# A graph layer with gathered rows on one core: the row gathers are made to wait for TensorE, and the two node tables are made in one pass

## The chip, the cores and the metric

The kernel runs on one core of a Trainium2 chip. The metric is the time on the device in microseconds (us), as the median of several runs. One execution was taken by the hardware profiler; its lines below name the engines PE (TensorE matmul), PEld (TensorE weight load), DVE (VectorE), ACT (ScalarE), POOL (GpSimd) and SP (SyncE). Every matmul of float32 shows as two matmuls and two weight loads in the trace, so counts of matmuls are twice those of the code.

## The reference: one message-passing layer

There are 6250 nodes with 128 features and 100000 edges, sorted by destination.

```python
msg_in = concatenate([x[src], x[dst], edge_features], axis=1)     # 128 + 128 + 4
h = silu(msg_in @ mW1 + mb1)
aggregated = segment_sum(h @ mW2 + mb2, dst, num_segments=N)
u = silu(concatenate([x, aggregated], axis=1) @ uW1 + ub1)
x = layernorm(x + layer_norm(x + u @ uW2 + ub2, ln_g, ln_b))
```

## The kernel before: two tables, then 98 groups of edges

**Split.** The first product is split by rows of mW1. Table A is x times the source part and table B is x times the destination part plus the bias. Both are written to DRAM (tab_a, tab_b), 49 tiles of 128 nodes each, in seven parts of up to eight tiles. Since the sum over edges is linear, h is summed per node first, and mW2 is folded into the node stage with a count of edges per node, deg.

**Start (L274 to L388).** POOL gathers the source rows of an edge group with `fetch(g)`: eight indirect DMAs of 128 rows each (L277). The first RAW = 4 groups are gathered from x itself, so that they need not wait for tab_a. PE turns x (`turn_x`, L330), multiplies part by part for A (`table(i0, n, 0)`, L350), ScalarE copies the result (L365), and SP writes it. After all of A come the destination lists, then the raw rows are turned (`turn_rows`, L357) and B is made part by part (L382) and written.

**Edge groups.** An edge group has 1024 edges in eight tiles; there are NG = 98. The destinations of one group span at most W = 96 nodes. Iteration g of the main loop runs, in the order written by hand for SP, PE, DVE and ACT:

- `fetch(g + AHEAD)` with AHEAD = 4 (POOL), and `load(g + 4)`, two short DMAs on SP (L553, L554)
- `hidden(g)`: VectorE adds the gathered rows to the product in PSUM (L598, tile s) and ScalarE applies silu (L599, tile h)
- `products(g + 2)`: PE, eight matmuls of the 96 B rows and the four edge features with a one-hot matrix (L583); raw groups add a product with the turned rows (L585)
- `node_matrix(g + 3)` and `edge_matrix(g + 1)`: the two one-hot matrices on VectorE (L558, L571). The first also leaves the group's degrees in a column of deg_g
- `add(g - 2)`: the sums and the degrees of the group are added to acc and deg (L622)
- `by_nodes(g)`: PE transposes the column of degrees (`degrees`, L604) and sums h per node with eight matmuls (L609, tile pt)

Every eighth group or so, a node batch of four tiles is threaded through the loop in steps (L476 to L526). The last two batches follow the last group.

**What orders the gathers.** POOL's order is not written by hand; a scheduler places its instructions, and the queue then runs in that order. The row tiles ga come from a pool of AHEAD + 2 = 6 buffers. A gather of group k therefore waits for the reader of group k - 6, which is the VectorE add L598 (for raw groups the products L585). Nothing else holds a gather back.

Of the kernel before, what the change touches and what calls it, by code (L numbers as in the profile page):

```python
# [8 lines left out]
F32 = mybir.dt.float32  # L9
# [9 lines left out]
P = 128  # L19
# [5 lines left out]
def kernel(  # L25
# [40 lines left out]
    nc = tc.nc  # L66
    N, H = x.shape
# [4 lines left out]
    G = 8  # L72
# [4 lines left out]
    NW = NP + W  # L77
    K1 = W + ED
    RB = 14
    AHEAD = 4  # L80
    LEAD = 4
    RAW = 4
    MADE = 3
    NQ = 4
    NM = 5
# [12 lines left out]
        return [(i, min(g, n - i)) for i in range(0, n, g)]  # L98


    LAST = 2
    batches = []
    first = (NT - 2 * LAST) % BT
# [5 lines left out]

    edges = ExitStack()  # L110
    edges.enter_context(tc.manual_schedule(engines={ENG.SP, ENG.PE, ENG.DVE, ENG.Activation}))
    gath = edges.enter_context(tc.tile_pool(name="gath", bufs=AHEAD + 2))
    work = edges.enter_context(tc.tile_pool(name="edge", bufs=2))

    tables = ExitStack()
# [3 lines left out]
    def wide():  # L119
        return tables_ps.tile([P, G, P], F32, name="wide")  # L120
# [67 lines left out]


    acc = consts.tile([P, NW], F32, name="acc")  # L190
    deg = consts.tile([1, NW], F32, name="deg")
    deg_g = consts.tile([W, NG], F32, name="deg_g")


    src_i = consts.tile([P, NG, G], I32, name="src_i")
# [18 lines left out]
    src_n = work.tile([P, GE], F32, name="s")[:NG]  # L214
    nc.vector.tensor_copy(src_n, src_l)
    by_lane(src_i, src_n)

    def destination_lists():
        base_c = work.tile([NG, 1], F32, name="base_c", bufs=1)
# [49 lines left out]
    def tiles_of(g):  # L269
        return min(G, -(-(E - g * GE) // P))  # L270

    def fetch(g):
        if g >= NG:
            return  # L274
        rows[g] = gath.tile([P, G, H], F32, name="ga")
        for i in range(tiles_of(g)):
            nc.gpsimd.indirect_dma_start(  # L277
                out=rows[g][:, i, :],
                out_offset=None,
                in_=x if g < RAW else tab_a[:, :],  # L280
                in_offset=bass.IndirectOffsetOnAxis(
                    ap=src_i[:, g, i : i + 1] if g else src_0[:, i : i + 1], axis=0
                ),
            )

    for g in range(RAW):
        fetch(g)


    turn = edges.enter_context(tc.tile_pool(name="turn", bufs=1))  # L290
# [29 lines left out]
    def by_node(t):  # L320
        return t[:NP].rearrange("(i p) f -> p i f", p=P)
# [5 lines left out]
    def turn_x(i0, n):  # L327
        pt = wide()
        for i in range(n):
            nc.tensor.transpose(pt[:, i, :], x_sb[:, i0 + i, :], ident)  # L330
        nc.scalar.copy(xT[:, i0 * P : (i0 + n) * P], pt[:, :n, :].rearrange("p i f -> p (i f)"))

    def load_bases(g):
        _, vals = nc.values_load_multi_w_load_instructions(
# [7 lines left out]
            bases[g + k] = v  # L342

    parts = groups(NT, G)

    def table(i0, n, half):
        pm = wide()
        for j in range(n):
            cols = slice((i0 + j) * P, (i0 + j + 1) * P)
            nc.tensor.matmul(pm[:, j, :], xT[:, cols], w1[:, half, :], start=True, stop=True)  # L350
        return pm[:, :n, :]
# [8 lines left out]
    turn_x(*parts[0])  # L360
    for k, (i0, n) in enumerate(parts):
        if k + 1 < len(parts):
            turn_x(*parts[k + 1])
        ta = tpool.tile([P, G, H], F32, name="t", bufs=2)
        nc.scalar.copy(ta[:, :n], table(i0, n, 0))  # L365
# [3 lines left out]
        nc.vector.memset(deg[:, cols], 0.0)  # L369
    for t in mv:  # L370
        nc.sync.dma_start(t[W:], mW1[2 * H :])
    attributes(0)
    destination_lists()
    attribute_rows(0)
    destinations(0)
    load_bases(0)
    for k, (i0, n) in enumerate(parts):
        if k < RAW:
            turn_rows(k)

        tb = x_sb[:, i0 : i0 + n, :]
        nc.vector.tensor_add(tb, table(i0, n, 1), b1[:, None, :].to_broadcast([P, n, H]))  # L382
        nc.sync.dma_start(by_node(tab_b)[:, i0 : i0 + n, :], tb)
    if E < NG * GE:
        pad = tpool.tile([ED, NG * GE - E], F32, name="pad")
        nc.vector.memset(pad, 0.0)
# [10 lines left out]


    w2u = consts.tile([P, H], F32, name="w2u")
    mb2u = consts.tile([1, H], F32, name="mb2u")  # L400
# [21 lines left out]
    def fuse_weights():  # L422
        pm = node_y()
        nc.tensor.transpose(pm[:, 0, :], raw_w["w2"], ident)
        w2T = work.tile([P, P], F32, name="w2T", bufs=1)
        nc.scalar.copy(w2T, pm[:, 0, :])
        nc.tensor.matmul(pm[:, 1, :], w2T, raw_w["u1a"], start=True, stop=True)
        nc.tensor.matmul(pm[0:1, 2, :], raw_w["mb2"], raw_w["u1a"], start=True, stop=True)
        nc.scalar.copy(w2u, pm[:, 1, :])
        nc.scalar.copy(mb2u, pm[0:1, 2, :])  # L430


    def node_batch(i0, n, work, new, y, final=False):
# [29 lines left out]
        sums, counts = acc[:, cols], deg[:, cols]  # L463
        if not final:

            acc_b, deg_b = new("acc_b"), new("deg_b", 1)
# [89 lines left out]
    def node_matrix(g):  # L556

        nc.vector.tensor_scalar(  # L558
            stbuf[g % NST][:W],
            near.pop(g),  # L560
            p_next,
            0.0,
            op0=OP.is_equal,
            op1=OP.add,
            accum_out=deg_g[:, g : g + 1],
        )

    def edge_matrix(g):
# [7 lines left out]
        )  # L576
        return oh

    def products(g):
        pre = rows_ps()  # L580
        st = stbuf[g % NST].rearrange("k (i c) -> k i c", i=G)
        for i in range(tiles_of(g)):
            nc.tensor.matmul(pre[:, i, :], st[:, i, :], mv[g % NM], start=True, stop=g >= RAW)  # L583
# [17 lines left out]

    def degrees(g):
        pt = ps.tile([P, 2 * W], F32, name="pt")
        nc.tensor.transpose(pt[0:1, W:], deg_g[:, g : g + 1], ident[:W, :W])  # L604
        return pt

    def sums(g, pt, h, oh, lo, hi):
        for i in range(lo, hi):
            nc.tensor.matmul(  # L609
                pt[:, :W], h[:, i, :], oh[:, i, :], start=i == 0, stop=i == tiles_of(g) - 1  # L610
            )

    def by_nodes(g, h, oh):

# [2 lines left out]
        return pt  # L617

    def add(g, pt):
        for to, of in ((acc, pt[:, :W]), (deg, pt[0:1, W:])):  # L620
            at = to[:, bass.ds(bases[g], W)]
            nc.vector.tensor_add(at, at, of)  # L622

    for g in range(LEAD):
        load(g)
# [4 lines left out]
    for g in range(NG):  # L630
        if g == 3:
            load_weights()
        if g == 4:
            destination_checks(node_y())
        if g == 5:
            fuse_weights()
        for c in range(1, NC):
            if g == max(1, c * EC // GE - 10):
                attributes(c)
            if g == max(1, c * EC // GE - 10) + 1:  # L640
                attribute_rows(c)
        if g + AHEAD >= RAW:
            fetch(g + AHEAD)
        if g + LEAD < NG:
            load(g + LEAD)
        last = g >= NG - 1
        if not last:
            h[g] = hidden(g)
        if g + 2 < NG:
            pre[g + 2] = products(g + 2)  # L650
        if g + MADE < NG:
            node_matrix(g + MADE)
        if g + 1 < NG:
            oh[g + 1] = edge_matrix(g + 1)
        if g - 2 in pt:
            add(g - 2, pt.pop(g - 2))
        if last:
            break
        pt[g] = by_nodes(g, h.pop(g), oh.pop(g))
        if g >= NG - 3:  # L660
            add(g - 1, pt.pop(g - 1))
        for i0, n, first in batches[:-1]:
            if g == (first if first >= NG - 3 else first + 1):
                running.append(node_batch(i0, n, *node_tiles(nodes, node_y)))
        for _ in range(2 if g >= NG - 6 else 1):
            advance(running)
# [58 lines left out]
def general(tc, tab_a, tab_b, src_i, rel, base_p, ea_d, p_col, ident, mW1, acc, deg):  # L725
# [9 lines left out]
    with ExitStack() as es:  # L735
# [84 lines left out]
        for i in range(NP // P):  # L820
            part = keep.tile([P, WR], F32, name="part")
            nc.sync.dma_start(part, sums[i * P : (i + 1) * P])
            p_s = ps.tile([P, P], F32, name="p_s")
            nc.tensor.transpose(p_s, part[:, :H], ident)
            nc.vector.tensor_copy(acc[:, i * P : (i + 1) * P], p_s)
            p_d = ps.tile([1, P], F32, name="p_d")
            nc.tensor.transpose(p_d, part[:, H : H + 1], ident)
            nc.vector.tensor_copy(deg[:, i * P : (i + 1) * P], p_d)


# [31 lines left out]
```

## Time and profile before

| | |
|---|---|
| three runs, median (lowest to highest) | 1332.58 us (1326.24 to 1334.16) |
| the profiled execution | 1330.48 us |
| its span, first to last instruction | 1328.7 us |
| granted TensorE clock, mean | 0.659 of full speed |
| gathers on POOL (L277), x782 | 739 us busy, 0.94 us each |
| edge products (L583), x1564 matmuls | 290.6 us busy, 0.33 us each |
| node sums (L609), x1564 matmuls | 285.4 us busy, 0.32 us each |
| DMA, mean | 67 GB/s |

Busy times are sums over an engine's instructions; matmuls are pipelined, so a matmul's own time is longer than the distance to the next. A row of waits reads: engine, tile and line that waited, what released it, total us, times, longest. "issue" as a releaser means that the engine waited for nothing that the profile shows; "remote" that the releaser could not be named.

### The profile page before, as it was taken

The numbers are of one execution on the slowest core, as the hardware profiler recorded it, in microseconds if no ns is written. First come the engines' busy times: TensorE is split into PE (matmuls) and PEld (weight loads), VectorE is DVE, ScalarE is ACT, GpSimd is POOL, SyncE is SP. The second block draws the span as 40 slices with busy tenths as digits, with TensorE's granted clock in tenths as the row PEclk, the third lists the DMA queues.
The fourth block names the chain that finished last, engine by engine and source line by source line (L and its number), as shares of the span: only waits on it lengthen the run. The fifth ranks groups of instructions, "written<-read, shape, count | busy, mean of one in ns | idle before, by whom it ended". The sixth has DMA issues, their size and how long they took to land.

```text
span 1328.7 us, 11483 instructions
## 1 busy us (share of the span) xinstructions
PE 719.1 (54%) x3802; PEld 613.8 (46%) x3802; DVE 478.3 (36%) x1019; ACT 242.6 (18%) x297; POOL 739.7 (56%) x790
## 2 busy tenths in 40 slices
PE   3547556348347348348357347348347347346494
PEld 3446456336336337346345246347236335344483
DVE  5033133324324324324323323324324323422563
ACT  0301012212212112112111210211221220210234
POOL 7245365665665665665664664664665664664600
PEclk9777656667567566567567666666667666766685
DMA  6453121221221221212121121221221221221200
GB/s 173 122 151 91 38 62 46 79 63 50 74 69 57 62 74 58 59 56 79 57 72 55 58 74 43 76 74 47 68 78 48 68 77 38 72 70 42 61 15 22
DMA packets 70221, 88.96 MB, mean 67 GB/s; under 512 B 20719, under 2 KB 51838, under 8 KB 70154
## 3 DMA queue, kind: packets, MB, share of 16 engines
q0 software_dynamic: 25024, 51.30, 13.6%
q1 hardware_dynamic: 40552, 34.96, 8.8%
q10 hardware_dynamic: 4578, 1.89, 0.6%
q8 instruction: 32, 0.52, 0.2%
q14 instruction: 35, 0.29, 0.1%
HBM read 76.71 MB, written 11.38 MB: 66 GB/s over the span
## 4 chain that ended last, share of the span: by engine, by line
PE 50%; issue 42%; DVE 3%; another core or an unknown queue 2%; DMA 1%; ACT 1%; DVEq 0%; SPq 0%; ACTq 0%
PE pre L583 19%; PE pt L609 19%; PE y L492 2%; PE wide L350 2%; PE y L476 1%; PE y L483 1%; PE y L477 1%; PE y L478 1%; PE pt L604 1%; PE pre L585 1%; DMA x_sb<-in_x_dram 1%; PE wide L330 0%; DVE st L450 0%; DVE st L558 0%
## 5 line engine op out<-in xcount | busy, mean ns | idle before, releaser
L277 POOL DMA_INDIRECT ga<-tab_a,src_i x750 | 708.0, 944 | 508.3 <-DVE s L598 240.9
L609 PE MATMUL pt<-oh,h 128*128 128x96 f32 x1564 | 285.4, 318 | 323.0 <-issue 314.8
L609 PEld LDWEIGHTS pt<-oh,h 128*128 128x128 f32 x1564 | 260.0, 237 | 345.4 <-issue 332.0
L583 PE MATMUL pre<-mv,st 100*128 100x128 f32 x1564 | 290.6, 334 | 173.9 <-issue 155.4
L583 PEld LDWEIGHTS pre<-mv,st 100*128 100x128 f32 x1564 | 257.2, 243 | 206.2 <-issue 200.8
L571 DVE TENSOR_TENSOR oh<-w_row,rel 128x768 f32<-128x768 f32 x98 | 93.1, 950 | 355.4 <-remote 343.4
L599 ACT ACTIVATE h<-s 128x1024 f32<-128x1024 f32 x93 | 98.1, 1055 | 657.0 <-DVE s L598 491.2
L598 DVE TENSOR_TENSOR s<-ga,pre 128x1024 f32<-128x1024 f32 x93 | 113.1, 1216 | 282.4 <-issue 193.1
L558 DVE TENSOR_SCALAR_CACHE_REDUCE st<-near,p_next 96x1024 f32<-96x1024 uint8 x98 | 124.0, 1267 | 5.0 <-DMA ea_d<-pad 4.6
L481 ACT ACTIVATE uT<-y,ub_col 128x512 f32<-128x512 f32 (+2 forms) x13 | 8.4, 645 | 253.7 <-PE y L478 235.4
L494 DVE TENSOR_TENSOR y<-y,xs 128x512 f32<-128x512 f32 (+2 forms) x13 | 8.4, 648 | 119.7 <-issue 95.3
L350 PE MATMUL wide<-w,xT 128*128 128x128 f32 x196 | 30.1, 314 | 18.8 <-issue 18.5
L599 ACT ACT_TABLE_LOAD x25 | 32.1, 1283 | 40.6 <-PE pre L585 38.8
L492 PEld LDWEIGHTS y<-u,uT 128*128 128x128 f32 x94 | 24.5, 318 | 29.1 <-issue 28.9
L350 PEld LDWEIGHTS wide<-w,xT 128*128 128x128 f32 x196 | 28.4, 229 | 18.8 <-issue 18.2
L492 PE MATMUL y<-u,uT 128*128 128x128 f32 x94 | 29.2, 437 | 14.6 <-issue 14.6
L604 PE MATMUL pt<-ident,deg_g 96*1 96x96 f32 x98 | 28.5, 291 | 15.6 <-issue 15.6
L456 ACT ACT_TABLE_LOAD x26 | 33.4, 1283 | 3.7 <-DVE mv L451 3.2
L277 POOL DMA_INDIRECT ga<-in_x_dram,src_i x24 | 23.0, 958 | 7.3 <-issue 7.3
L483 PE MATMUL y<-ub_row,ones 1*128 1x512 f32 (+2 forms) x26 | 19.8, 832 | 10.7 <-issue 10.6
L622 DVE TENSOR_TENSOR acc<-acc,pt 128x96 f32 x98 | 23.6, 241 | 1.7 <-PE pt L609 1.7
L622 DVE TENSOR_TENSOR deg<-deg,pt 1x96 f32 x98 | 23.0, 235 | 0.0
(117 smaller groups left out, 391.1 us busy)
## 6 DMA issues: line engine op xcount, KB each, us to landing
ga<-tab_a,src_i POOLq DMA_INDIRECT x750
near<-near_d SPq DMA_DIRECT2D x24, 384.0 KB
mv<-tab_b SPq DMA_DIRECT2D x98, 48.0 KB
tab_a<-t SPq DMA_DIRECT2D x6, 512.0 KB
tab_b<-x_sb SPq DMA_DIRECT2D x6, 512.0 KB
xs<-in_x_dram SPq DMA_DIRECT2D x11, 256.0 KB
out_dram<-z SPq DMA_DIRECT2D x11, 256.0 KB
st<-ea_d SPq DMA_DIRECT2D x98, 16.0 KB
```

What stands on the lines that cost most here:

```text
L277: nc.gpsimd.indirect_dma_start(out=rows[g][:, i, :], out_offset=None, in_=x if g < RAW else tab_a[:, :], in_offset=bass.IndirectOffsetOnAx ...
L350: nc.tensor.matmul(pm[:, j, :], xT[:, cols], w1[:, half, :], start=True, stop=True)
L456: nc.scalar.activation(r[:, :n], mv[:, :n, 1], AF.Sqrt, bias=eps)
L492: nc.tensor.matmul(y[:, i, :], by_p[:, :, i], u2, start=False, stop=i == n - 1)
L558: nc.vector.tensor_scalar(stbuf[g % NST][:W], near.pop(g), p_next, 0.0, op0=OP.is_equal, op1=OP.add, accum_out=deg_g[:, g : g + 1],)
L571: nc.vector.tensor_tensor(oh, w_row[:, None, :].to_broadcast([P, G, W]), rel[:, g, :, None].to_broadcast([P, G, W]), op=OP.is_equal,)
L583: nc.tensor.matmul(pre[:, i, :], st[:, i, :], mv[g % NM], start=True, stop=g >= RAW)
L598: nc.vector.tensor_add(s[:, :n], ga[:, :n], ps[:, :n])
L599: nc.scalar.activation(h[:, :n], s[:, :n], AF.Silu)
L604: nc.tensor.transpose(pt[0:1, W:], deg_g[:, g : g + 1], ident[:W, :W])
L609: nc.tensor.matmul(pt[:, :W], h[:, i, :], oh[:, i, :], start=i == 0, stop=i == tiles_of(g) - 1)
L622: nc.vector.tensor_add(at, at, of)
```

## The change

Six things are done.

1. `fetch(g)` is now called two groups ahead, at the end of iteration g - 2, and takes instructions of PE to wait for. With one, the first gather of the group waits for it; with two, the first waits for the first and the fifth for the second. From group CLOSE = 14 on these are the first matmul of products(g) and the first matmul of the sums of group g - 2. Groups 5 to 13 wait for the first product of group g - 5. The pool of row tiles still has six buffers.
2. Groups 0 to 4 are raw (RAW = 5). Their gathers are called between the parts of the tables: group 1 after the first turned part, 2 after the table products of parts 0 and 1, 3 after parts 2 and 3, 4 after part 4. Group 4 is turned later, inside the main loop (`turn_late`).
3. A and B of a part are made by one matmul of width 256, and both are copied out and written before the next part. `destination_lists` moves into this loop, after part 2.
4. The degrees are kept in columns 0, 32, 64 and 96 of a tile for four groups, so that one transpose serves four groups; the four rows are then added to deg one by one. deg has 97 rows, of which four are used, and mb2u likewise.
5. deg is cleared at once ahead of the tables.
6. Only `fetch` differs on POOL. As the scheduler places them, the other six gathers of a group are not held behind the two that wait. A typical stretch of POOL's order in the changed kernel is, by group, with P where a gather waits for PE: 43 43 43 42P 43 43 43 43P 44 44 44 43P 44 44 44P 44 45. In each group the first gather in line waits for the VectorE add of group g - 6. Group 5 has seven gathers ahead of the one that waits.

```diff
-    AHEAD = 4
+    AHEAD = 2
+    CLOSE = 14
-    RAW = 4
+    RAW = 5
...
-    def fetch(g):
-        if g >= NG:
-            return
+    def fetch(g, *after):
...
-            nc.gpsimd.indirect_dma_start(
+            ins = nc.gpsimd.indirect_dma_start(
...
+            part, at = divmod(i * len(after), G)
+            if after and at == 0:
+                tc.add_manual_dep(
+                    ins.ins,
+                    after[part].ins.name,
...
-    for g in range(RAW):
-        fetch(g)
+    fetch(0)
...
+    def turn_late(g):
+        for lo in range(0, G, BT):
+            px = node_y()
+            for i in range(BT):
+                nc.tensor.transpose(px[:, i, :], rows[g][:, lo + i, :], ident)
+            nc.vector.tensor_copy(rows[g][:, lo : lo + BT], px)
+
+    fetch(1, turn_x(*parts[0]))
     for k, (i0, n) in enumerate(parts):
         if k + 1 < len(parts):
             turn_x(*parts[k + 1])
+
+        tb = x_sb[:, i0 : i0 + n, :]
         ta = tpool.tile([P, G, H], F32, name="t", bufs=2)
-        nc.scalar.copy(ta[:, :n], table(i0, n, 0))
+        for j0, m in groups(n, G // 2):
+            pm = wide().rearrange("p (i s) f -> p i s f", s=2)
+            for j in range(m):
+                cols = slice((i0 + j0 + j) * P, (i0 + j0 + j + 1) * P)
+                ins = nc.tensor.matmul(pm[:, j], xT[:, cols], w1, start=True, stop=True)
+            own = slice(j0, j0 + m)
+            nc.scalar.copy(ta[:, own], pm[:, :m, 0, :])
+            nc.vector.tensor_add(
+                tb[:, own], pm[:, :m, 1, :], b1[:, None, :].to_broadcast([P, m, H])
+            )
         nc.sync.dma_start(by_node(tab_a)[:, i0 : i0 + n, :], ta[:, :n])
+        nc.sync.dma_start(by_node(tab_b)[:, i0 : i0 + n, :], tb)
+        table.append(ins)
+        if k == 1:
+            fetch(2, *table)
+        if k == 2:
+            destination_lists()
+        if k == 3:
+            fetch(3, *table[2:])
...
+        if k == 4:
+            fetch(4, table[4])
...
-        nc.tensor.transpose(pt[0:1, W:], deg_g[:, g : g + 1], ident[:W, :W])
+        if g % DQ == 0:
+            nc.tensor.transpose(pt[:DR, W:], deg_q[g // DQ % 2], ident[:W, :W])
...
-        for to, of in ((acc, pt[:, :W]), (deg, pt[0:1, W:])):
-            at = to[:, bass.ds(bases[g], W)]
-            nc.vector.tensor_add(at, at, of)
+        at = acc[:, bass.ds(bases[g], W)]
+        nc.vector.tensor_add(at, at, pt[:, :W])
+        if g % DQ == 0:
+            for k in range(min(DQ, NG - g)):
+                row = slice(32 * k, 32 * k + 1)
+                at = deg[row, bass.ds(bases[g + k], W)]
+                nc.vector.tensor_add(at, at, pt[row, W:])
...
-        if g + AHEAD >= RAW:
-            fetch(g + AHEAD)
...
+        if TURNED <= g + 2 < RAW:
+            turn_late(g + 2)
...
         pt[g] = by_nodes(g, h.pop(g), oh.pop(g))
+        ahead = g + AHEAD
+        if CLOSE <= ahead < NG:
+            fetch(ahead, begun[ahead], summing[g])
+        elif RAW <= ahead < NG:
+            fetch(ahead, begun[ahead - 5])
```

More of the change, by code (lines that the diff above doesn't have):

```diff
@@ L98, in groups @@
         return [(i, min(g, n - i)) for i in range(0, n, g)]
+    TURNED = 4
+    DQ = 4
+    DR = 32 * (DQ - 1) + 1
     LAST = 2
@@ L111 @@
     edges.enter_context(tc.manual_schedule(engines={ENG.SP, ENG.PE, ENG.DVE, ENG.Activation}))
-    gath = edges.enter_context(tc.tile_pool(name="gath", bufs=AHEAD + 2))
+    gath = edges.enter_context(tc.tile_pool(name="gath", bufs=6))
     work = edges.enter_context(tc.tile_pool(name="edge", bufs=2))
@@ L190 @@
     acc = consts.tile([P, NW], F32, name="acc")
-    deg = consts.tile([1, NW], F32, name="deg")
-    deg_g = consts.tile([W, NG], F32, name="deg_g")
+    deg = consts.tile([DR, NW], F32, name="deg")
+    deg_q = [consts.tile([W, DR], F32, name=f"deg_q{k}") for k in range(2)]
     src_i = consts.tile([P, NG, G], I32, name="src_i")
@@ L216 @@
     by_lane(src_i, src_n)
+    for t in [deg] + deg_q:
+        nc.vector.memset(t, 0.0)
     def destination_lists():
@@ L284, in fetch @@
             )
-    for g in range(RAW):
-        fetch(g)
+            part, at = divmod(i * len(after), G)
[3 more added lines that the diff above has]
+                    after[part].ins.name,
+                    mybir.DependencyInfo(
+                        mybir.DependencyClass.Sync, mybir.DependencyReason.DATA
+                    ),
+                    reason="TensorE keeps up with the gathers",
+                )
+    fetch(0)
     turn = edges.enter_context(tc.tile_pool(name="turn", bufs=1))
@@ L329, in turn_x @@
         for i in range(n):
-            nc.tensor.transpose(pt[:, i, :], x_sb[:, i0 + i, :], ident)
+            ins = nc.tensor.transpose(pt[:, i, :], x_sb[:, i0 + i, :], ident)
         nc.scalar.copy(xT[:, i0 * P : (i0 + n) * P], pt[:, :n, :].rearrange("p i f -> p (i f)"))
+        return ins
     def load_bases(g):
@@ L344 @@
     parts = groups(NT, G)
[L346 to L351, printed above, removed]
+    table = []
     def turn_rows(g):
@@ L358, in turn_rows @@
         nc.vector.tensor_copy(rows[g], px)
-    turn_x(*parts[0])
+    def turn_late(g):
[5 more added lines that the diff above has]
+    fetch(1, turn_x(*parts[0]))
     for k, (i0, n) in enumerate(parts):
@@ L363 @@
             turn_x(*parts[k + 1])
+        tb = x_sb[:, i0 : i0 + n, :]
         ta = tpool.tile([P, G, H], F32, name="t", bufs=2)
-        nc.scalar.copy(ta[:, :n], table(i0, n, 0))
-        nc.sync.dma_start(by_node(tab_a)[:, i0 : i0 + n, :], ta[:, :n])
+        for j0, m in groups(n, G // 2):
[7 more added lines that the diff above has]
+                tb[:, own], pm[:, :m, 1, :], b1[:, None, :].to_broadcast([P, m, H])
+            )
+        nc.sync.dma_start(by_node(tab_a)[:, i0 : i0 + n, :], ta[:, :n])
+        nc.sync.dma_start(by_node(tab_b)[:, i0 : i0 + n, :], tb)
[6 more added lines that the diff above has]
+            fetch(3, *table[2:])
         cols = slice(i0 * P, NW if i0 + n == NT else (i0 + n) * P)
         nc.vector.memset(acc[:, cols], 0.0)
-        nc.vector.memset(deg[:, cols], 0.0)
+        if k == 4:
+            fetch(4, table[4])
     for t in mv:
@@ L372 @@
     attributes(0)
-    destination_lists()
     attribute_rows(0)
@@ L376 @@
     load_bases(0)
[L377 to L383, printed above, removed]
+    for g in range(TURNED):
+        turn_rows(g)
     if E < NG * GE:
@@ L399 @@
     w2u = consts.tile([P, H], F32, name="w2u")
-    mb2u = consts.tile([1, H], F32, name="mb2u")
+    mb2u = consts.tile([DR, H], F32, name="mb2u")
     u1x = consts.tile([P, H], F32, name="u1x")
@@ L429, in fuse_weights @@
         nc.scalar.copy(w2u, pm[:, 1, :])
-        nc.scalar.copy(mb2u, pm[0:1, 2, :])
+        nc.vector.memset(mb2u, 0.0)
+        for k in range(DQ):
+            nc.scalar.copy(mb2u[32 * k : 32 * k + 1], pm[0:1, 2, :])
     def node_batch(i0, n, work, new, y, final=False):
@@ L464, in node_batch @@
         if not final:
-            acc_b, deg_b = new("acc_b"), new("deg_b", 1)
+            acc_b, deg_b = new("acc_b"), new("deg_b", DR)
             nc.scalar.copy(flat(acc_b), sums)
@@ L564, in node_matrix @@
             op1=OP.add,
-            accum_out=deg_g[:, g : g + 1],
+            accum_out=deg_q[g // DQ % 2][:, g % DQ * 32 : g % DQ * 32 + 1],
         )
@@ L577, in edge_matrix @@
         return oh
+    begun, summing = {}, {}
     def products(g):
@@ L582, in products @@
         for i in range(tiles_of(g)):
-            nc.tensor.matmul(pre[:, i, :], st[:, i, :], mv[g % NM], start=True, stop=g >= RAW)
+            ins = nc.tensor.matmul(pre[:, i, :], st[:, i, :], mv[g % NM], start=True, stop=g >= RAW)
+            begun.setdefault(g, ins)
             if g < RAW:
@@ L608, in sums @@
         for i in range(lo, hi):
-            nc.tensor.matmul(
+            ins = nc.tensor.matmul(
                 pt[:, :W], h[:, i, :], oh[:, i, :], start=i == 0, stop=i == tiles_of(g) - 1
             )
+            summing.setdefault(g, ins)
     def by_nodes(g, h, oh):
@@ L827, in general @@
             nc.tensor.transpose(p_d, part[:, H : H + 1], ident)
-            nc.vector.tensor_copy(deg[:, i * P : (i + 1) * P], p_d)
+            nc.vector.memset(deg[:, i * P : (i + 1) * P], 0.0)
+            nc.vector.tensor_copy(deg[0:1, i * P : (i + 1) * P], p_d)
 _INS = [
```

## The prediction

> **What bounds the kernel now.** I read the page first, then the table of waits for GpSimd (POOL), then busy time by stretch around one stop of the gathers, then the time line of POOL and TensorE (PE) there.
>
> ```profile
> PE 719.1 (54%) x3802; PEld 613.8 (46%) x3802; DVE 478.3 (36%) x1019; ACT 242.6 (18%) x297; POOL 739.7 (56%) x790
> PE 50%; issue 42%; DVE 3%; another core or an unknown queue 2%; DMA 1%; ACT 1%; DVEq 0%; SPq 0%; ACTq 0%
> POOL ga L277 <- DVE s L598: 240.9, 33, 18.2
> POOL ga L277 <- issue: 214.3, 695, 1.6
> ACT t L365 <- remote: 29.1, 1, 29.1
> ```
>
> No engine is busy above 56%, and 42% of the chain that ends last is "issue" on PE: PE waits, but for nothing that the profile shows. POOL is closer to a limit than its 56% say: a gather is busy 0.944 us and the next starts 1.2475 us after it, so the 782 gathers take 976 us if they never stop. They do stop: 240.9 us for the VectorE add L598, which frees a row buffer. That add waits for PE. So the question is why PE falls behind.
>
> ```profile
> 600.50:609.00 8.50, 8.50 (x66) 7.37 (x66) 2.59 (x5) 3.69 (x4) 6.37 (x8) 0.97 0.48 129
> 609.00:617.00 8.00, 4.31 (x11) 2.23 (x10) 1.27 (x3) 0.00 (x0) 6.15 (x7) 0.64 0.23 64
> 617.00:620.70 3.70, 1.19 (x3) 1.16 (x4) 0.00 (x0) 0.00 (x0) 0.94 (x1) 0.50 0.12 35
> 620.70:632.50 11.80, 11.78 (x87) 11.59 (x87) 11.04 (x27) 4.98 (x5) 5.37 (x6) 0.82 0.27 81
> 632.50:655.00 22.50, 3.91 (x14) 3.15 (x12) 6.82 (x19) 3.92 (x4) 17.02 (x19) 0.56 0.22 64
> 655.00:659.30 4.30, 1.11 (x3) 1.15 (x4) 0.00 (x0) 0.00 (x0) 0.26 (x1) 0.50 0.05 15
> ```
>
> The columns are the stretch, its length, busy time (instructions) of PE, weight loads, VectorE, ScalarE, POOL, then PE's clock, the DMA share and GB/s. While gathers run, PE first does 66 matmuls in 8.5 us; then it crawls: 14 in 22.5 us. When POOL stops, PE recovers. The time lines give the edges:
>
> ```profile
> 653.73 0.32 PE L609 MATMUL pt<-oh,h 128*128 128x96 f32 x1 [2.48 <-issue]
> 655.83 0.37 PE L583 MATMUL pre<-mv,st 100*128 100x128 f32 x1 [1.79 <-issue]
> 659.33 2.94 PE L583 MATMUL pre<-mv,st 100*128 100x128 f32 x13 [0.33 <-issue]
> 654.32 0.94 POOL L277 DMA_INDIRECT ga<-tab_a,src_i  x1 [0.30 <-issue]
> 660.98 0.94 POOL L277 DMA_INDIRECT ga<-tab_a,src_i  x1 [5.72 <-DVE s L598]
> ```
>
> POOL's last gather ends at 655.3, PE is out of the crawl about 2.7 us later, POOL restarts at 661.0. I counted this over all 38 stops. Nearly every run of gathers, of 16 (20 us) or 24 (30 us), holds 67 to 79 matmuls, about 60 of them in its first 7 to 11 us. After the two stops of 1.6 us (at 481.5 and 680.6) PE stayed in the crawl; after one of 3.1 us (at 126.7) it did not. So each stop longer than about 2.7 us buys PE about 73 matmuls, however long the run that follows. The trace does not say what PE lacks in the crawl; that it is tied to the gathers follows only from the timing.
>
> The account by POOL: at 107.0 us groups 0 to 5 are gathered. The other 734 gathers x 1.2475 = 916, stops 237, and 69 from the last gather (1259.5) to the end: 107 + 916 + 237 + 69 = 1329, the span. From 263.6 to 1232.4 there are 616 gathers: 968.8 - 768.5 = 200 us of stops in 77 groups, 2.6 us a group.
>
> **The change, part by part.** *Gathers wait for PE.* As built, each group keeps six gathers without a wait on PE. One waits for the first product of its group, usually seventh in line; one, three or four places into the next group, waits for the first sum of two groups before. Everything behind them on POOL's queue is only gathers. Buffers no longer bind. A group needs 16 + 16 matmuls, 202/98 = 2.1 for node batches and now a quarter of a transpose: 34.3. From a restart, the wait met after 16 gathers (20 us) needs about 70 matmuls where a run gives 67 to 79, so about two are left: a stop of 2.7 + 2 x 0.225 (L583 at half clock, 3.62 us for 16) = 3.2 us for 2 groups, 1.6 a group. If it is passed, the next is 5 gathers later and needs 87, 14 beyond 73: 2.7 + 14 x 0.225 = 5.9 us for 2.6 groups, 2.2 a group. Mean 1.9; one stop in five or so too short to help (1.6 us, as the two seen) adds 0.2. I take 2.1 against 2.6: 84 groups x 2.1 = 176. Bounds: 1.5 (every stop at the first place) and, if nothing improves, 2.6.
>
> [...]
>
> [...] More stops mean more restarts at half rate; the rows show 0.50 around each stop already. At half rate 34.3 matmuls take 7.7 us, under the 10.0 us of a group's eight gathers, so only the matmuls between recovery and release count, and those I priced at 0.225. [...]
>
> *Going from far ahead to two ahead.* At group 14 the gathers are some five groups ahead of PE. PE catches up about two groups at 4 us (624 to 636 shows about 4 us a group at full pace): one stop of about 9 us, more than is usual by that much.
>
> *End.* Now POOL ends 69 us before the kernel, with seven sums still to do. After it, the last gather waits for the first sum of group 95. In the trace that group's transpose L604 starts at 1290.4, 38.3 us before the end. One gather later POOL is done: 37 us of tail.
>
> *Tables.* Before, 32 raw gathers run from 3 to 43 us, PE crawls from 22.9, and the first copy of A waits 29.1 us (the ScalarE row above); B follows and the edges start at 100. After, A and B are one matmul of width 256: 98 instead of 196, so less of the 60-matmul credit. But six gathers each of groups 2 and 3 are free of PE, so POOL runs from 3 to about 38, stops some 11 us for the third table part, and PE then needs about 67 matmuls x 0.25 = 17 us: loop over at 70. From there the trace has 5.6 us to the near load (62.9 to 68.5), its landing is not seen (3 to 5, estimated), and the first loads of a group take 2.8 us to the first product (97.3 to 100.1), with the turned rows (four copies of 1.23 us) in between: about 15, edges at 85 (76 to 95). tab_a lies ready at about 72, and seven gathers of group 5 need no product, so at 85 POOL has 47 gathers behind it. SP is passed by seven table writes of B, 512 KB each, which took 8.4 us of issue for five; they lie in PE's time.
>
> *Early stops* of groups 5 to 13: 38, as before's five stops from 107 to 264 (3.1, 18.2, 5.7, 5.6, 5.6), because the destination checks and raw products remain.
>
> *Small edits.* 73 transposes fewer (0.29 us each, 21 us of PE) lie under the gathers; as credit, one stop. The sums of degrees are as many (98 x 0.235), four together, 0.94 us on VectorE, which idles. Clearing deg in one piece costs by L369 (0.91 for 1024) 5.7 us, as before. Group 4 raw: 16 products more (0.25 us, 4 us) and eight transposes and two copies, inside the early stops. Three copies of 0.25 us once.
>
> **Sum**, from 85: 735 gathers x 1.2475 = 917; 38; 9; 176; 37. 85 + 917 + 38 + 9 + 176 + 37 = 1262 of span. The profiled execution took 1330.5 for a span of 1328.7, the median is 1332.6: add 4, 1266.
>
> **Rivals.** *Shorter stops, no fewer us:* POOL stops more often and still 2.6 us a group. [...] Against: two stops of 5.7 and one of 12 (717) bought the same 71 to 76. 1266 + 42 = 1308. *The waits do not bind:* six of eight gathers don't wait; if buffers still bind, tail 69 and stops 2.6, start gained: 1266 + 42 + 32 - 9 = 1331. Against: the first-product wait comes four groups sooner than the buffer's. *All better:* every stop at 16 gathers (84 x 1.5 = 126) and early stops 25: 1266 - 50 - 13 = 1203. *Slower:* a short stop gives only part of the credit. Stops are now cut off as soon as PE moves; if one of 3.2 us buys 40 matmuls, 1.2 groups, that is 2.7 a group and short misses come on top: at 3.3, 1367. It decides from (1333 - 1266)/84 + 2.1 = 2.9 us a group on. Against: after 3.1 us at 126.7 came 64 matmuls, 50 at full pace; that is one case, with raw products.
>
> **How the numbers follow.** Forecast 0.60 (own range 1235 to 1300), shorter stops 0.15, not binding 0.07, all better 0.09, slower 0.09. A measurement can tell about 1% from no change (1319 to 1346). Faster: 0.58 + 0.11 + 0.01 + 0.09 = 0.79; within 1%: 0.02 + 0.04 + 0.05 + 0.01 = 0.12; slower 0.09. Range 1205 to 1325, reaching into "all better" and past "shorter stops"; outside lie the slower case, most of "not binding" and half of "all better", two in ten.
>
> **What would show it.** POOL's waits on PE L617 and L645 in place of VectorE's add; 35 to 50 stops of 3 to 6 us, under 180 us in all after group 14; crawls of 2 to 12 us, not 22; first edge product at about 85; the last gather 37 us before the end. Wrong if many stops are under 2.7 us, if runs hold clearly fewer than 67 matmuls, or if the tables end after 95.

## The result: 1212.7 us, and the profile after

The changed kernel takes 1212.70 us (median of 4 runs, 1208.80 to 1214.94) against 1333.37 us before (1326.24 to 1345.47, 4 runs): a ratio of 0.9083, 95% interval 0.9013 to 0.9154. The profiled execution took 1208.8 us for a span of 1207.0 us. One thing has to be said at once: on other occasions the same kernel before took 1017 to 1019 us, the changed one 1026, and the gain was gone; both conditions are taken up below.

The page after, engine totals and the chain that ended last:

```profile
PE 735.1 (61%) x3655; PEld 656.4 (54%) x3655; DVE 488.3 (40%) x1023; ACT 244.6 (20%) x306; POOL 740.8 (61%) x790
issue 40%; POOL 27%; another core or an unknown queue 10%; DVE 9%; PE 9%; DMA 3%; ACT 1%; SPq 1%; DVEq 0%; POOLq 0%; ACTq 0%
```

PE fell from half of the chain to 9%, and POOL stands with 27% where it had none: the chain now runs through the gathers. "issue" is still 40%. POOL's waits, with total us, times and longest:

```profile
POOL ga L282 <- remote: 138.7, 55, 4.0
POOL ga L282 <- PE pre L617: 37.2, 8, 20.0
POOL ga L282 <- PE pt L645: 10.3, 6, 3.4
```

The wait for VectorE's add, 240.9 us before, is gone. "remote" are releases that could not be named; 55 of them, none over 4.0 us. Busy time by stretch around two stops (the columns as before: PE, weight loads, VectorE, ScalarE, POOL, PE's clock, DMA share, GB/s) and the time line of the first stop:

```profile
566.00:576.00 10.00, 6.93 (x41) 6.77 (x41) 1.68 (x4) 1.76 (x4) 7.56 (x9) 0.76 0.26 65
576.00:586.60 10.60, 4.83 (x26) 4.17 (x26) 2.27 (x6) 2.02 (x3) 7.88 (x9) 0.58 0.19 51
586.60:589.80 3.20, 1.15 (x3) 0.89 (x4) 1.52 (x2) 0.21 (x1) 0.00 (x0) 0.50 0.09 20
589.80:599.50 9.70, 9.14 (x43) 7.36 (x42) 2.20 (x5) 2.39 (x5) 7.54 (x8) 0.75 0.48 140
599.50:609.80 10.30, 3.47 (x15) 2.76 (x16) 6.50 (x12) 1.06 (x1) 7.55 (x8) 0.60 0.22 57
```

```profile
585.37 0.95 POOL L282 DMA_INDIRECT ga<-tab_a,src_i  x1 [0.30 <-issue]
589.81 0.94 POOL L282 DMA_INDIRECT ga<-tab_a,src_i  x1 [3.49 <-remote]
```

A run of 16 gathers (589.8 to 609.8) holds 58 matmuls, 43 of them in the first half; the stop before it holds 3. PE still crawls, but for ten microseconds instead of twenty, and POOL restarts as soon as PE moves (PE from 589.50 us on without gaps, POOL at 589.81). Over the whole trace from 221.2 us on there are 46 stops with 124.1 us, 2.7 us each on average and none over 3.7. Before, from 263.6 us on, there were 31 with 199.7 us, 6.4 each. Per group that is 1.50 us (83 groups) against 2.6.

### The profile page after: what moved, and what is told of

It reads as the page before. It is cut to its first block, busy times and chain, and to the rows that moved or that the text cites. A ratio compares the mean times of both kernels' runs of the same rounds, so it can differ in the third digit from the quotient of the medians.

```text
span 1207.0 us, 11413 instructions
## 1 busy us (share of the span) xinstructions
PE 735.1 (61%) x3655; PEld 656.4 (54%) x3655; DVE 488.3 (40%) x1023; ACT 244.6 (20%) x306; POOL 740.8 (61%) x790
## 4 chain that ended last, share of the span: by engine, by line
issue 40%; POOL 27%; another core or an unknown queue 10%; DVE 9%; PE 9%; DMA 3%; ACT 1%; SPq 1%; DVEq 0%; POOLq 0%; ACTq 0%
POOL ga L282 27%; PE pt L645 2%; PE pre L617 2%; PE wide L387 2%; DVE oh L603 2%; DVE s L633 1%; DVE st L590 1%; DMA ga<-tab_a,src_i 1%; DVE st L482 1%; DMA x_sb<-in_x_dram 1%; DVE y L526 1%; PE wide L344 1%; DVE mv L483 0%; DMA w<-in_L_gnn_mW_dram 0%
## 5 line engine op out<-in xcount | busy, mean ns | idle before, releaser
L617 PE MATMUL pre<-mv,st 100*128 100x128 f32 x1564 | 318.2, 366 | 189.8 <-issue 150.6
L645 PE MATMUL pt<-oh,h 128*128 128x96 f32 x1564 | 305.9, 349 | 209.2 <-issue 200.1
L645 PEld LDWEIGHTS pt<-oh,h 128*128 128x128 f32 x1564 | 286.0, 266 | 229.1 <-issue 220.7
L617 PEld LDWEIGHTS pre<-mv,st 100*128 100x128 f32 x1564 | 288.8, 274 | 212.6 <-issue 179.8
L590 DVE TENSOR_SCALAR_CACHE_REDUCE st<-near,p_next 96x1024 f32<-96x1024 uint8 x98 | 124.2, 1269 | 6.2 <-DMA near<-near_d 6.0
L282 POOL DMA_INDIRECT ga<-in_x_dram,src_i x32 | 30.3, 947 | 17.4 <-issue 8.2
L387 PE MATMUL wide<-w,xT 128*128 128x256 f32 x98 | 26.8, 432 | 10.7 <-DVE x_sb L390 8.0
L387 PEld LDWEIGHTS wide<-w,xT 128*128 128x128 f32 x98 | 21.1, 222 | 15.0 <-DVE x_sb L390 8.6
L483 DVE BATCH_NORM_AGGREGATE mv<-st 128x2 f32<-128x6 f32 x98 | 17.8, 182 | 13.1 <-remote 5.1
L620 PE MATMUL pre<-w,ga 128*128 128x128 f32 x80 | 19.8, 332 | 2.2 <-issue 2.2
```

What stands on the lines that cost most here:

```text
L282: ins = nc.gpsimd.indirect_dma_start(out=rows[g][:, i, :], out_offset=None, in_=x if g < RAW else tab_a[:, :], in_offset=bass.IndirectOffs ...
L387: ins = nc.tensor.matmul(pm[:, j], xT[:, cols], w1, start=True, stop=True)
L590: nc.vector.tensor_scalar(stbuf[g % NST][:W], near.pop(g), p_next, 0.0, op0=OP.is_equal, op1=OP.add, accum_out=deg_q[g // DQ % 2][:, g % D ...
L617: ins = nc.tensor.matmul(pre[:, i, :], st[:, i, :], mv[g % NM], start=True, stop=g >= RAW)
L645: ins = nc.tensor.matmul(pt[:, :W], h[:, i, :], oh[:, i, :], start=i == 0, stop=i == tiles_of(g) - 1)
```

## The experiments

Four things were open: is it the waits that brought the gain, what is the crawl tied to, how much does a pause of POOL buy, and does PE need whole pauses or only wider gaps between gathers.

### The waits alone, and the kernel without them: where nothing crawls

Three kernels, one part each. e1 is the changed kernel with its waits left out:

```diff
-            fetch(ahead, begun[ahead], summing[g])
+            fetch(ahead)
...
-            fetch(ahead, begun[ahead - 5])
+            fetch(ahead)
```

e2 is the kernel before with `fetch(g, *after)`, AHEAD = 2, CLOSE = 14, six buffers and the calls at the end of the loop from the change, and nothing else of it. e3 is the kernel before with fewer row buffers:

```diff
-    gath = edges.enter_context(tc.tile_pool(name="gath", bufs=AHEAD + 2))
+    gath = edges.enter_context(tc.tile_pool(name="gath", bufs=4))
```

> The changed kernel with every wait of a gather on TensorE taken out of groups 5 to 97; tables, degrees and call order as changed; a gather waits only for its row buffer. Theory (a running gather starves TensorE's issue, each stop of about 3 us buys 60 to 70 matmuls, and the waits cut the stops from 6.4 to 2.7 us): the stops come back to 2.6 us a group (+91), the tail to 69 us (+37), the pause at group 14 goes (-20): 1213 + 108 = about 1320, stops on VectorE's add. Rival (the gain is the start and the smaller instruction count, not the waits): about 1225.

> The kernel before with only the waits: gathers called two groups ahead and held as in the changed kernel from group 14 on; tables one after the other, four raw groups, one transpose of degrees per group. Theory: stops 1.5 us a group, tail about 32, edges at 100 as before: 1333 - 91 - 37 + 12 = about 1217 to 1235. Rival (start and instruction count): 1310 to 1325.

> The kernel before with four row buffers in place of six, nothing else: gathers run two groups less far ahead, but a stop still ends only with VectorE's add. Theory: it is how a stop ends that counts, not how far ahead the gathers are; stops stay at 2.6 us a group, only the tail loses two groups (about 8 us): 1310 to 1335. Rival (running less far ahead is what helps): about 1230 to 1250.

Measured: the kernel before 1019.07 us (17 runs, 1017.43 to 1022.09), e1 1021.19 (ratio 1.0019, 1.0006 to 1.0032), e2 1022.76 (1.0038, 1.0024 to 1.0051), e3 1039.19 (1.0201, 1.0180 to 1.0221). Every expectation missed, the kernel before included, which ran 314 us shorter than on record. In these traces POOL hardly stops: 10.5 us in two stops in e1, 6.8 us in two in e2, 23.6 us in one in e3, all before 75 us (a stop is counted here without the 0.30 us that POOL pauses between any two gathers). The rest is 782 gathers at a median pitch of 1.25 us. So without the crawl POOL's queue is the bound and waits for PE buy nothing. e1 and e3 were not run where there is a crawl: for e1 a block of the last kernel below stands in, but what e3 was to tell, whether it is enough that gathers run less far ahead, stays untested.

The changed kernel itself and e1 again, on a second chip:

> The changed kernel, unaltered, beside the kernel before on one chip. Two cases are told apart by the kernel before itself. If TensorE crawls beside the gathers here (the kernel before near 1333 us), my theory gives 1213 us, a ratio of 0.91, with some 46 stops of POOL near 2.7 us after group 14. If it does not crawl (the kernel before near 1019 us, as in the first runs), nothing makes POOL stop, the sum is start + 782 gathers x 1.25 us + tail, and the change can only bring the earlier start of the gathers and the shorter tail: 990 to 1015 us, ratio 0.97 to 1.00. A rival says that the waits cost stops of their own where there is no crawl: 1025 to 1045.

> The changed kernel with the waits of its gathers on TensorE left out, so that only the six row buffers hold the gathers back. With the crawl (kernel before near 1333): my theory gives 1300 to 1325, since long runs of gathers, long stops and the long tail come back; the rival that the tables and the third raw group bring the gain gives 1215 to 1240. Without the crawl: the same time as the changed kernel with its waits, within 0.5%, about 1020.

Measured: before 1017.29 us, changed 1025.78 (ratio 1.0081, 1.0064 to 1.0098), without waits 1022.03 (1.0037, 1.0018 to 1.0057). I had expected 0.97 to 1.00 for the changed kernel; the rival, 1025 to 1045 through stops that the waits make, came in. Its trace has the last gather end at 994.2 us, 31.6 us before the end, with four stops of 11.0 us in all, every one before 75 us (up to 4.9 us, on the first products). The waits cost 3.7 us of the 8.5; the rest lies in the other edits, the tables among them, and was not taken apart, since there is no trace of the kernel before in this condition.

### What the crawl is tied to

A kernel of independent matmuls (two records each, as all f32 products here) runs seven phases, each beside something else:

```python
phase(lambda: small(320), lambda: [gather(land[0], i) for i in range(K)], ...)
phase(lambda: small(320), lambda: [nc.gpsimd.memset(work, float(i)) for i in range(K)], ...)
phase(lambda: small(320), lambda: [nc.sync.dma_start(land[1][:, i, :], ...) for i in range(K)], ...)
phase(lambda: small(320), lambda: [nc.gpsimd.dma_start(land[0][:, i, :], ...) for i in range(K)], ...)
phase(lambda: small(320), lambda: [gather(land[1], i, 32) for i in range(K)], ...)
phase(lambda: wide(120), lambda: [gather(land[0], i) for i in range(K)], ...)
```

> Not the layer: matmuls with no dependence on anything, beside other work, in phases; the output is a copy of x. First 320 float32 matmuls (640 in the trace) alone, then 320 beside 40 gathers, beside 40 fills on GpSimd of 1200 columns, beside 40 plain loads of 64 KB on SP, beside 40 plain loads of 64 KB issued by GpSimd, beside 40 gathers of 32 rows, then 120 matmuls of 512 columns beside 40 gathers. Theory (gathers, not data or GpSimd's work, hold back TensorE's issue): alone, fills and SP's loads 0.11 to 0.23 us a matmul; beside gathers 60 to 70 at that pace and then one in 1.4 to 2.5 us until about 2.7 us after the last gather; the wide ones as few per us as the narrow. GpSimd's plain loads and small gathers are open: if each issue counts they crawl too, if descriptors count the small gathers crawl less. Rival (DMA traffic): SP's loads crawl as well, small gathers a quarter. Rival (GpSimd's work): the fills crawl too.

> Only a measurement: independent matmuls in seven phases, alone, beside 40 gathers, beside 40 fills by POOL, beside 40 plain loads from SP, beside 40 plain loads from POOL, beside 40 gathers of 32 rows, and 120 matmuls of width 512 beside 40 gathers; the output is a copy of the input, not the reference's. If the kernel before shows the crawl on this chip: about 60 matmuls at 0.11 us after the first gather, then one per 1.4 to 2.5 us until the gathers end, and none of it beside the fills; the wide ones crawl at the same rate per instruction if it is their issue that is starved, and at a quarter of it or less in time lost if it is their data. If it does not: 0.109 us in every phase, as before.

> The independent matmuls in seven phases once more; the output is a copy of the input, not the reference's. With the crawl (the kernel before near 1333 us): beside 128-row gathers about 60 matmuls at 0.11 us, then one per 1.4 to 2.5 us, and none of it beside POOL's fills. Without it: 0.109 us in every phase, 546 us in all.

The first two ran on the two chips above: 545.8 and 545.99 us, no crawl in any phase. Stretch over the gathers in the first (the kernel uses only PE and POOL; columns PE, weight loads, POOL, clock, DMA share, GB/s):

```profile
85.00:135.00 50.00, 50.00 (x451) 50.00 (x450) 37.58 (x40) 1.00 0.21 52
```

The third ran where the kernel before took 1327.48 us (7 runs), and took 653.74 us:

```profile
84.00:94.00 10.00, 10.00 (x92) 9.97 (x90) 7.69 (x8) 1.00 0.16 48
94.00:134.00 40.00, 9.58 (x32) 7.05 (x31) 30.18 (x33) 0.56 0.19 52
200.00:244.00 44.00, 44.00 (x396) 44.00 (x395) 41.80 (x39) 1.00 0.01 1
280.00:310.00 30.00, 30.00 (x271) 30.00 (x270) 0.00 (x0) 1.00 0.54 163
345.00:364.00 19.00, 19.00 (x173) 19.00 (x172) 19.00 (x37) 1.00 0.43 126
422.00:461.00 39.00, 6.88 (x23) 4.98 (x22) 28.88 (x34) 0.56 0.06 15
544.00:580.00 36.00, 36.00 (x86) 15.91 (x85) 27.17 (x29) 1.00 0.18 51
580.00:594.00 14.00, 5.13 (x7) 1.43 (x6) 10.60 (x12) 0.62 0.18 52
```

In order: 128-row gathers, 92 matmuls at full pace and then 32 in 40 us; POOL's fills, nothing; SP's loads at 163 GB/s, nothing; plain loads issued by POOL at 126 GB/s, nothing; 32-row gathers, the same crawl at 15 GB/s; wide matmuls, 86 at full pace and then 7 in 14 us. PE has no data to wait for here, the clock stands at 1.00 until the crawl is there, and bandwidth plays no part. Counted from the first gather, 90 matmuls run at full pace beside 128-row gathers (in 10 us), 70 beside 32-row gathers (in 8 us) and 83 wide ones (in 36 us), where about 60 were expected. The times differ by a factor of more than four, the counts by less than a third: the crawl comes nearer to a fixed number of instructions than to a fixed time. That settles, for this condition, what the prediction could only read from the timing: beside indirect DMAs on POOL, PE falls into the crawl after some 70 to 90 matmuls.

What it is that PE lacks is not settled. Two more readings go with it. The deep crawl has a pace of its own, one matmul every 2.80 us, for narrow and for wide matmuls; on the way there the starts lie mostly 0.70, 1.40 or 2.10 us apart (time lines of the third run, beside 128-row gathers):

```profile
117.31 0.37 PE L95 MATMUL acc<-xs 128*128 128x128 f32 x1 [2.43 <-issue]
120.11 0.37 PE L95 MATMUL acc<-xs 128*128 128x128 f32 x1 [2.43 <-issue]
591.99 1.01 PE L101 MATMUL acc<-xs 128*128 128x512 f32 x1 [1.79 <-issue]
594.79 1.01 PE L101 MATMUL acc<-xs 128*128 128x512 f32 x1 [1.79 <-issue]
```

The other is the DMA queue q8, of the kind "instruction": 32 blocks with 0.52 MB in the trace before, for 3802 matmuls, and 31 for 3655 after. That they are PE's is read from these counts, 119 and 118 matmuls a block. First the third run from 84 to 134 us, with 124 matmuls, then the first run from 85 to 135 us, with 451:

```profile
q8 instruction: 1, 0.02, 0.1%
q8 instruction: 4, 0.07, 0.5%
```

So with the crawl, too, a block goes with about as many matmuls: 124 to one here, 113 without it. And no block marks the crawl's end: in the trace before, q8 moved nothing from 630 to 678 us, and in that time PE left one crawl after POOL's stop, did 68 matmuls in 13.3 us (658.6 to 671.9) and went into the next (9 in the 6.1 us after that). What delays PE, no run shows.

### The waits alone, with the crawl

On the same occasion, the kernel before once more and e2 unchanged:

> The kernel before, unaltered, for its trace on this chip. If TensorE crawls beside the gathers here: near 1333 us, 38 stops of POOL, 237 us of them. If it does not: near 1018 us; POOL's 782 gathers at 1.25 us take 978 us, one stop of 2 to 6 us before 70 us where table A is awaited, and about 31 us of tail, which would leave the change 8 us slower by its 11.5 us of stops (1.6, 3.9 and 4.8 us before 75 us) against these 2 to 6.

> The kernel before with nothing but the waits of the gathers on TensorE and the two groups in front taken from the change; its tables, its four raw groups, its sums of degrees stay. With the crawl: my theory gives 1217 to 1250, nearly all of the gain, the rival that the tables bring it gives 1310 to 1340. Without the crawl: 1020 to 1025, 0.4% above the kernel before, as on the first chip.

Measured: the kernel before, taken once more, 1335.72 us (37 stops of POOL with 286 us, tail 68 us; without the two in the start 244 us, where the trace on record has 237), and 1327.48 us as the median of the 7 runs beside; e2 1227.78 us, ratio 0.9266 (0.9217 to 0.9315), as my theory had it. POOL's waits of e2:

```profile
POOL ga L277 <- remote: 124.0, 49, 3.6
POOL ga L277 <- PE pre L595: 44.2, 5, 19.7
```

The add is gone here too. From 240 us on 51 stops take 124.8 us for 659 gathers, 1.51 us a group, and the tail is 34.1 us: much the same as in the changed kernel. So the waits alone, with the call two groups ahead that goes with them, bring 7.3 of the 9.2%. What remains was measured on two occasions, whose kernels before differ by 6 us: 15 us by the times, some 24 by the ratios. Most of it goes with the start: e2's first edge product is at 99.3 us, the changed kernel's at 82.3.

### What a pause buys

A stream of matmuls beside runs of 16 gathers with one fill between them, then single gathers each with a fill, then bf16 products:

```python
runs = [gather] * 20
for n in (1200, 2400, 3600, 600, 1800, 4800, 3000, 7200, 2400):
    runs += [lambda n=n: fill(n)] + [gather] * 16
...
beside(lambda: small(300), [gather, lambda: fill(600)] * 20)
...
beside(lambda: half(500), [gather] * 16)
```

> Only a measurement (output a copy of the input): a long stream of independent matmuls on TensorE, beside runs of 16 gathers parted by one POOL fill of 1.1, 2.2, 3.3, 0.6, 1.7, 4.4, 2.7, 6.6 and 2.2 us; then 20 gathers with a fill of 0.6 us behind each; then 16 gathers beside bf16 products, which are one instruction where an f32 product is two. With the crawl (kernel before near 1333 us), my theory: a pause below about 2 us leaves TensorE in the crawl, from about 2.7 us on each pause buys the same 60 to 100 matmuls, and more than 4 us buys no more. Rival: what a pause buys grows with its length, 20 to 30 matmuls per us. Beside bf16 products the crawl starts after as many instructions, so twice as many products. Without the crawl: 0.109 us a matmul throughout.

Measured, on a fourth chip (kernel before 1338.36 us): 564.1 us. Rows of five stretches (PE, weight loads, VectorE, POOL, clock, DMA share, GB/s):

```profile
190.50:194.60 4.10, 0.47 (x2) 0.58 (x2) 0.00 (x0) 4.10 (x1) 0.50 0.06 16
194.60:214.50 19.90, 2.87 (x8) 2.30 (x8) 0.00 (x0) 15.16 (x18) 0.50 0.19 49
237.00:243.10 6.10, 2.78 (x6) 1.46 (x6) 0.00 (x0) 6.10 (x1) 0.50 0.04 11
243.10:253.10 10.00, 10.00 (x78) 10.00 (x77) 0.00 (x0) 7.57 (x8) 0.85 0.17 46
434.40:469.20 34.80, 34.80 (x314) 34.80 (x314) 0.00 (x0) 31.31 (x40) 1.00 0.15 38
```

My bound of 2.7 us fell: after pauses of 0.6 to 4.1 us the next run held 7 to 13 matmuls; only 6.1 us brought PE back (93). Then a pause of 2.1 us, met after ten instead of twenty microseconds of crawl, gave a run with 34. The rival (so many matmuls per us of pause) fares no better. What seems to count is how deep the crawl has become: the gap between matmuls grows from 0.4 to 2.8 us as it goes on. That rests on one run with one order of pauses. Beside bf16 products, one record each, 67 ran at full pace (in 4 us), against 90 records, that is 45 products, of f32: 1.5 times as many products, where twice as many were expected. So it is somewhat nearer to records that are counted than to products. The last row was not expected by anyone: with a fill of 0.6 us behind every gather there is no crawl at all (314 matmuls in 34.8 us).

### Gaps in place of pauses

So a last kernel: the changed one without waits on PE (as e1), POOL in program order, and a fill behind each gather from group 14 on, in four blocks of 21 groups.

```diff
+    FILLS = (240, 1, 400, 120)
+    spare = consts.tile([P, 400], F32, name="spare")
...
+            if g >= CLOSE:
+                nc.gpsimd.memset(spare[:, : FILLS[(g - CLOSE) // 21]], 0.0)
```

> The changed kernel without any wait of the gathers on TensorE, with a fill by POOL behind each gather from group 14 on, in four blocks of 21 groups: 240, 1, 400 and 120 columns (about 0.32, 0.12, 0.45 and 0.22 us by the two fills of 1.12 and 0.62 us measured), POOL in program order. With the crawl: if a gap between gathers is what TensorE needs, and these are long enough, POOL has no stops in that block and 168 gathers take 241, 207, 263 and 224 us (a gather and its fill of 0.62 us took 1.73 us, so 1.23 + what the fill is over 0.12); all four together then end near 1160 us, below both kernels. In a block whose fill is too short TensorE stays in the crawl, POOL stops on VectorE's adds, and it costs 2.6 us a group or more as in the kernel before, 55 us for the block; all four too short: 1380. Rival: only whole pauses of 2.7 us or more help, and the fills merely cost their time. Without the crawl: 1020 us plus what the fills add to the pitch, 80 to 130 us.

Measured: 1278.73 us, ratio 0.9616 (0.9581 to 0.9652), the kernel before 1330.11 us (7 runs). This was the first chip again, where the kernel before had taken 1019 us: the crawl is not a property of the chip. POOL's waits in the block with 1 column and in the block with 400:

```profile
POOL ga L284 <- DVE s L637: 55.5, 9, 14.5
POOL ga L284 <- issue: 32.0, 157, 1.4
```

```profile
POOL ga L284 <- issue: 28.1, 167, 0.7
POOL ga L284 <- DVE y L540: 0.2, 1, 0.2
```

| columns | fill, us | median pitch of gathers | stops in the block | us a group beyond 8 x pitch |
|---|---|---|---|---|
| 1 | 0.12 | 1.25 | 57.7 us | 2.75 |
| 120 | 0.21 | 1.33 | 20.5 us | 0.98 |
| 240 | 0.32 | 1.43 | 0.8 us | 0.04 |
| 400 | 0.45 | 1.56 | 0.5 us | 0.02 |

The blocks of 240 and 400 columns took 241 and 263 us, as expected; those of 1 and 120 columns took 268 and 242, where 207 and 224 were expected of fills that are long enough, and the total of 1160 was missed. The 1-column fill goes into the pause that POOL makes between gathers anyway (0.30 us without it; with it 0.11 of fill and 0.19 of pause), and that block is the changed kernel without its waits: 2.75 us of stops a group, as before the change, against 1.50 with them. From 0.32 us on there is next to no stop, so the rival, that only whole pauses help, is out. But the price is the same: 8 x 1.43 + 0.04 = 11.5 us a group against 8 x 1.2475 + 1.50 = 11.5. The total is above 1212.7 because the blocks of 1 and of 400 columns took some 27 and 21 us more than 21 groups at 11.5 us, and the tail is 63 us. A kernel with one fill between 120 and 240 columns, or with 120 and the waits, was not run; none of those that were run beats the changed one where there is a crawl, and none the kernel before where there is none.

## Why the prediction came out, step by step

**The bound: right, in the condition of the record.** Gathers put PE into a crawl, POOL's stops end it, and the waits change when POOL stops: e2 and the 1-column block show the waits, the streams show the crawl. The prediction took the crawl for a property of the program. It isn't: the same program on the same chip ran with it and without it. That the run on record fell where there is a crawl was luck; elsewhere the same change takes 0.8% more time.

**PE's issue.** With the crawl, PE ran 32 matmuls in 40 us beside gathers with no data to wait for (third run of the streams), and the waits left 1.50 us of stops a group where it had been 2.6. Without the crawl it ran 451 in 50 us beside the same gathers (first run).

**The half clock.** More stops (58 against 38 in the whole trace) did not lower the granted clock: its mean is 0.678 against 0.659 before.

**Steady stops: the term that was mis-sized.** "I take 2.1 against 2.6: 84 groups x 2.1 = 176" measured 124, 52 us less and nearly all of the miss. I had reckoned that a wait that is passed leads to a stop of 5.9 us at the next one, with about 14 matmuls of it still to do, and that one stop in five would be too short to help. No stop was over 3.7 us, and only four of the 46 were under 2, three of which were too short to help (the next stop came within 8 us). A stop buys less than I said (about 60 matmuls, not 73), which is the direction of the slower rival, but it comes after 1.8 groups and is over at 2.7 us. The value is that of "all better", which I had given 0.09.

**Catching up at group 14.** 9 us forecast, 20.0 measured (the longest wait on L617 above): PE did 107 matmuls in it, three groups, not two.

**The rest.** First edge product 85 forecast, 82.3 measured; gathers from there 917 and 915.7; early stops 38 (36.7 without the 0.30 us that belongs to each gather) and 29; tail 37 and 31.6. The 3 to 5 us for the landing of the near load, a part of the 85, were an estimate that no trace shows; after the change, the load was issued at 74.60 and the VectorE instruction that waited for it (L590) began at 80.25, 5.7 us later. From 84.3 us: 84.3 + 915.7 + 173.2 of stops (29 + 20 + 124) + 31.6 = 1204.8, and 2.2 us of small delays make the span of 1207.0.

**Rivals.** "Shorter stops, no fewer us" and "the waits do not bind" are out by 1.50 against 2.6 us a group; the 42 us that both add to the forecast (84 groups x 0.5) no run of the changed kernel shows: its stops came out 52 us under the forecast's 176. "Slower" needed 2.9.

**What stays open.** Why gathers hold PE back on one occasion and not on another. All runs of one occasion agreed: 17 at 1017 to 1022 us, then 8 at 1016 to 1020; 7 at 1320 to 1344, later 7 at 1319 to 1333. One sign goes with it: the list of DMA issues gives a landing time for the gathers only where there is no crawl (first line: the changed kernel on record; second: on the second chip):

```profile
ga<-tab_a,src_i POOLq DMA_INDIRECT x742
```

```profile
ga<-tab_a,src_i POOLq DMA_INDIRECT x742, 2.6
```

With the crawl no gather has a landing time in the list (the kernel before and the changed one on record). Such gaps go with the occasion and not with the crawl itself: POOL's plain loads in the streams, beside which nothing crawls, lack their time too (third run, then first):

```profile
land<-in_x_dram POOLq DMA_DIRECT2D x40, 64.0 KB
land<-in_x_dram POOLq DMA_DIRECT2D x40, 64.0 KB, 2.3
```

Every execution on record comes with a recorded span and clock, so none shows the kernel without recording. Whether the crawl and the missing times have one cause, and whether recording itself slows PE, no run here tells. If it does, the gain is there only while the profiler records.

## What to carry to other kernels

When an engine is idle for "issue" beside another engine's indirect DMAs, count its instructions per run of DMAs: nearly the same number, whatever their size, was the sign of this crawl (90 and 83 at full pace, narrow and wide), and what helped here was to pause the DMAs early and often, before the crawl is deep (2.7 us after every 1.8 groups), or to widen the gap between them (a pitch of 1.43 instead of 1.25 us). The waits alone cost 0.4% where there is no crawl and brought 7.3% where there was. Before tuning to such an effect, see whether the kernel has a second level of time at all (here 1018 and 1333 us); a change is then to be judged at both.

## What the runs showed of the hardware that was not expected

- The crawl comes and goes on one chip: 1019 and 1330 us for the same kernel.
- An indirect DMA of 32 rows holds PE back as one of 128 does (23 matmuls in 39 us and 32 in 40), and takes POOL 0.86 against 0.94 us: a quarter of the rows saves less than a tenth of the time.
- A deep crawl has one pace, a matmul every 2.80 us, narrow or wide (third run of the streams).
- Fills behind each gather: 0.62 us in the streams left no crawl (314 matmuls in 34.8 us). In the layer, 0.32 us (pitch 1.43 instead of 1.25 us) left 0.04 us of stops a group, 0.21 us 0.98 and 0.12 us 2.75, at an unchanged pitch of 1.25 us.
